# Planned cost of plain tap transfers halved for products 1 and 3, and twenty idle transposes ahead of the first product

## The chip, the cores and the metric

The kernel runs on one core of one Trainium2 chip. The metric is the device time in microseconds (us) of one execution. Engines are named as in the profile: PE is TensorE (matmuls; PEld its weight loads), DVE VectorE, ACT ScalarE, POOL GpSimd, SP SyncE, which issues most transfers. GpSimd also issues the transfers that add into their destination.

## What is computed

A pre-norm transformer block on x of 2 sequences by 1024 tokens by 1024 channels, in float32:

```
x = x + attention(layernorm(x))
x = x + ffn(layernorm(x))

attention(h):  h -> convolution over tokens, width 3, 1024 -> 768 channels
               split into q, k, v of 256; 16 heads of 64; causal softmax
               inside blocks of 128 tokens; out projection; 256 -> 1024
ffn(h):        h @ W_base.T + b_base + four gated low-rank experts
```

The change lies wholly in the first stage, the layer norm and the convolution, which takes the first 235 us of the 770.

## The kernel before, in words

**The convolution as six products.** Four neighbouring output tokens are computed together from six combinations of input tokens, so the convolution becomes six matrix products, numbered v = 0 to 5. Product v multiplies a combination of the tokens (called `v` in the trace, 128 channels by 512 token groups) with a combination of the three taps of the filter (called `u`, 128 by 768). Products 0 and 5 use one tap as it is. Products 1 and 2 share a combination of all three taps, and so do 3 and 4. The products run in the order 0, 5, 1, 2, 3, 4. Each walks over eight blocks of 128 input channels, here called steps d = 0 to 7, and in each step over six blocks of output channels.

**Three matmuls for one.** Each operand is split into a high and a low part, and `three` (line 137) adds high x high, high x low and low x high. The high part comes from ACT, the low part from DVE: `u_hi` (line 441) and `u_lo` (line 445) for taps, `v_hi` (line 500) and `v_lo` (line 504) for tokens. A step is 18 matmuls. Since a step's first two matmuls use only the high part of the tap, PE can begin a step and then wait for `u_lo`.

**How the taps of products 1 and 3 are made.** `load_g` (lines 414 to 416) issues two plain transfers on SP's queue, 384 KB each. For product 1, `sum_g` (line 423) then adds the second and the third tap onto the first in two transfers on POOL's queue, the second waiting for the first. `combine` (line 431 for product 1, lines 435 and 436 for product 3) turns the two tiles into the taps of two products on DVE; `u_hi` and `u_lo` follow. For product 3 one `sum_g` follows after `scale_g` on ACT.

**How the tokens of products 1 to 4 are made.** `tokens_sum` (lines 487 to 490) makes both token combinations for two steps at once. It is four DVE instructions in a row; in the planner it is one piece of 4.7 us.

**The order is planned when the program is built.** Each piece of work is an `Op` with an engine, a planned duration, a due time, a lead, the pieces it comes after, and a lag before its result counts (3.3 for transfers). `trace` (line 289) is a list scheduler: again and again it takes, over all engines, the piece that can start first. On one engine it goes through the pieces by due time and keeps the earliest start, so a piece that is due earlier loses to one that can start sooner. A start is the latest of: the engine is free, due minus lead plus the lateness so far (`late`, how far PE's plan has slipped), and the predecessors' ends with their lags. All transfers share one planned engine "DMA", one at a time. Only the order leaves the planner: the program issues the pieces in the order of their planned starts, each engine carries out its own pieces strictly in that order on the chip, and the planned times themselves appear nowhere in the program. Tiles of tags such as `t3` (23 buffers for taps) are handed out in the same order.

**Due times that matter here.** `begin_chunk` (line 751) plans the tap of step d. In the plan, step d of product 1 is due at 97.2 + 4.3 d. From that, `load_g` is due 34.0 earlier with a lead of 6.0, the first sum 28.0 and the second 21.0 earlier without lead, `combine` 9.5, `u_hi` 5.0 and `u_lo` 2.5 earlier. `tokens_sum` for steps d and d+1 is due 9.0 earlier with the large lead of 22.0.

**The start.** `keep_busy` (line 698) issues transposes of the identity into an unused PSUM bank, `idle`. Line 705 runs 64 of them while the first tokens load. Then come 32 transposes of the first four token tiles (`tr`, line 385), then the first product.

Of the kernel before, what the change touches and what calls it, by code (L numbers as in the profile page):

```python
# [39 lines left out]
def preln_block_kernel(  # L40
# [197 lines left out]
    def bank(name):  # L238
        return ps_m.tile([P, JN], F32, tag="m", name=name)
# [393 lines left out]
    DVE, ACT, PE, DMA = "DVE", "ACT", "PE", "DMA"  # L633

    def load(due, lead, f, *args, takes=1.1, after=()):
        return Op(DMA, takes, due, lead, after, lambda: f(*args), lag=3.3)
# [11 lines left out]
    seen = {}  # L648

    def turn(i, h):  # L650

        due = at[0]
        if h == 0:
            how = HOW[i]
            if how == "scalar":
                o = Op(ACT, 1.3, due - 8.0, 8.0, [loaded[i]], partial(ln_sum, i))
                o = Op(ACT, 1.2, due - 6.0, 8.0, [o], partial(ln_square, i))
                o = Op(DVE, 0.1, due - 4.5, 8.0, [o], partial(ln_variance, i), lag=1.8)
            else:
                lag = 1.0 if how == "vector" else 1.8  # L660
                o = Op(DVE, 1.6, due - 5.5, 8.0, [loaded[i]], partial(ln_stats, i), lag=lag)
            e, us = (DVE, 0.75) if how == "vector" else (ACT, 1.15)
            seen[i] = Op(e, us, due - 2.2, 8.0, [o], partial(ln_scale, i))
        o = Op(
            PE, TR, due, 6.0, [seen[i], banks[-2] if len(banks) > 7 else None],
            partial(transpose, i, h),
        )
        if (i, h) == (8, 0):

            gone["even"] = Op(  # L670
                DMA, 0.01, due - 2.0, 50.0, [seen["tr", j, 1] for j in range(8)], even_tokens
            )
        after = [o] + ([gone["even"]] if i > 7 else [])
        seen["tr", i, h] = o
        banks.append(Op(ACT, 0.52, due + TR, 8.0, after, partial(transposed, i, h)))
        at[0] += TR
        seen[i, h] = banks[-1]

    def weights_due(v, d, due, after):
        o = Op(ACT, 0.76, due - 5.0, 12.0, [after], partial(u_hi, v, d))  # L680
        return Op(DVE, 0.89, due - 2.5, 12.0, [o, after], partial(u_lo, v, d))
# [16 lines left out]
    def keep_busy(n):  # L698
        if not idle:
            idle.append(bank("idle"))  # L700
        for _ in range(n):
            nc.tensor.transpose(idle[0][:, :P], ident, ident)
# [7 lines left out]
    def evacuated(v, c, due):  # L710
        o = gone[v, c] = Op(ACT, 0.55 if v < 4 else 0.85, due, 3.0, [last], partial(evacuate, v, c))
        gone["m", v, c] = load(due, 3.0, spill, v, c, after=[o], takes=0.7)

    for q, (v, n, dc) in enumerate(units):
        base = 0 if v == 0 else 8
        took = [seen.get((base + 4 * n + i, dc // 4)) for i in range(4)]
        if None in took:
            for i in range(4):
                turn(base + 4 * n + i, dc // 4)
            took = [seen[base + 4 * n + i, dc // 4] for i in range(4)]  # L720
        due = at[0]
        o = Op(DVE, 1.28, due - 5.5, 9.0, took, partial(unit_sum, q))
        o = Op(ACT, 0.55, due - 3.5, 9.0, [o], partial(unit_hi, q))
        side = Op(DVE, 0.64, due - 1.5, 9.0, [o], partial(unit_lo, q))
        for i in range(2):
            d = dc + i
            if n == 0:
                if v == 5:
                    gs[5, d] = load(at[0] - 12.0, 12.0, load_g, 5, d)
                ready[v, d] = weights_due(v, d, at[0], gs[v, d])  # L730
            for c in range(NCC):
                after = [last, side, ready[v, d]]
                if v == 5 and n == 0 and d == 0:
                    after.append(gone[0, max(0, c - 1)])
                last = Op(
                    PE, HALF / NCC, at[0], 6.0, after, partial(multiply_unit, q, i, c), lag=0.0
                )
                at[0] += HALF / NCC
            for j in between.get((q, i), []):
                turn(*j)  # L740
        if (n, dc) == (1, NDC - 2):
            for c in range(NCC):
                evacuated(v, c, at[0] + 0.1 * c)
# [6 lines left out]

    def begin_chunk(v, d, due):
        if v == 1:
            o = load(due - 34.0, 6.0, load_g, v, d, takes=2.2)
            for k in (1, 2):
                o = load(due - 35.0 + 7.0 * k, 0.0, sum_g, v, d, k, takes=2.2, after=[o])
            o = Op(DVE, 0.9, due - 9.5, 9.0, [o], partial(combine, v, d))
        elif v == 3:
            o = load(due - 28.0, 6.0, load_g, v, d, takes=2.2)
            o = Op(ACT, 0.76, due - 21.0, 0.0, [o], partial(scale_g, v, d))
            o = load(due - 21.0, 0.0, sum_g, v, d, 0, takes=2.2, after=[o])  # L760
            o = Op(DVE, 1.8, due - 9.5, 9.0, [o], partial(combine, v, d))
        if v in (1, 3):
            gone["g", v, d] = gone["g", v + 1, d] = o
        ready[v, d] = weights_due(v, d, due, gone["g", v, d])
# [16 lines left out]
    for v, dc in [(v, dc) for v in (1, 2, 3) for dc in range(0, NDC, 2)] + [(4, 0), (4, 2)]:  # L781
        if (v, dc) == (2, 0):

            for r in range(4):
                load(
                    at[0] + r, 3.0, nc.sync.dma_start, mask[r::4], causal[ts(r, P // 4)],
                    after=[last],
                )
            Op(DVE, 1.0, at[0], 3.0, [last], gather_experts)
        if (v, dc) == (3, 0):  # L790
            Op(ACT, 0.3, at[0], 3.0, [last], router_bias)
        side = begin_step(v, dc, at[0])
        for d in (dc, dc + 1):
            begin_chunk(v, d, at[0])
            for c in range(NCC):
                last = product(v, d, c, side)
        if dc == NDC - 2:
            for c in range(NCC):
                evacuated(v, c, at[0] + 0.1 * c)

    sides = {}
    for dc in (4, 6):
        sides[dc] = begin_step(4, dc, at[0])
        for d in (dc, dc + 1):
            begin_chunk(4, d, at[0])
# [5 lines left out]
    for c in range(NCC):  # L811
# [7 lines left out]
        o = Op(DVE, 2.7, at[0] + 1.0, 6.0, [got, gone[4, c]], partial(tokens_join, 0, c))  # L819
        o = Op(ACT, 0.6, at[0] + 4.0, 6.0, [o], partial(tokens_hi, 0, c))  # L820
# [432 lines left out]
    d = {}  # L1253
# [364 lines left out]
```

## Time and profile before

| | |
|---|---|
| median of 3 runs | 773.37 us (772.95 to 774.4) |
| the profiled execution's own time | 771.87 us |
| its span, first to last instruction | 770.1 us |
| PE busy | 757.3 us, 98% of the span |
| DVE, ACT, POOL busy | 71%, 52%, 20% |
| mean granted PE clock | 0.996 |
| first stage ends, first `pq` matmul | 234.93 us |

A profile line such as `L445 DVE TENSOR_TENSOR u<-g,u ... x1` names the source line, the engine, the operation and output <- inputs, then shapes and count. In a timeline the first two numbers are the start and the duration in us, and a bracket at the end gives the idle time before the piece and who ended it. "Granted clock" is the share of full clock that the chip's throttle gave PE. Durations of PE instructions contain their pipeline's drain, so neighbours overlap.

### The profile page before, as it was taken

The page shows a single profiled execution, that of the slowest core. Times are in us where ns is not written, and L with a number is a line of the kernel's source. Part 1 is how long each engine was busy: PE and PEld are TensorE (multiplying, and loading weights), DVE is VectorE, ACT ScalarE, POOL GpSimd, SP SyncE. Part 2 cuts the span into 40 slices and gives each one's busy share as a digit, 9 for nine tenths or more (in the row PEclk, how much of TensorE's full clock was granted, in tenths as well). Part 3 has the DMA queues.
Part 4 walks back from the last instruction along what each step waited for, and adds up shares of the span by engine and source line. Part 5 has one row for each costly group of instructions (what it writes and reads, how often), then busy time and mean ns, then how long its engine had stood idle before and what let it go on. Part 6 is the DMA issues. An engine that isn't in the chain of part 4 may idle for free.

```text
span 770.1 us, 13080 instructions
## 1 busy us (share of the span) xinstructions
PE 757.3 (98%) x4928; PEld 676.8 (88%) x4928; DVE 545.8 (71%) x1027; ACT 401.3 (52%) x1015; POOL 157.5 (20%) x138
## 2 busy tenths in 40 slices
PE   6999999999999999999999999999999999999998
PEld 6999978888888888888888887889999999999997
DVE  7788899799667899787787788687444454444532
ACT  6888344564746988888777989832101010110110
POOL 3224322210000304111213013532112111221000
PEclk9999999999999999999999999999999999999999
DMA  9937993996752111030131646750223112311011
GB/s 344 360 102 204 240 259 84 289 292 131 237 156 83 42 54 31 22 117 23 40 94 52 184 154 221 269 234 28 91 74 110 54 55 91 129 55 55 29 55 54
DMA packets 53662, 100.17 MB, mean 130 GB/s; under 512 B 4526, under 2 KB 23742, under 8 KB 53600
## 3 DMA queue, kind: packets, MB, share of 16 engines
q1 hardware_dynamic: 49872, 89.35, 33.4%
q0 software_dynamic: 3728, 10.00, 7.2%
q8 instruction: 38, 0.62, 0.3%
q14 instruction: 24, 0.20, 0.1%
HBM read 73.12 MB, written 26.21 MB: 129 GB/s over the span
## 4 chain that ended last, share of the span: by engine, by line
PE 91%; DVE 6%; issue 2%; DMA 1%; ACT 1%; POOL 0%; SPq 0%; DVEq 0%
PE py L140 24%; PE pm L140 22%; PE pq L140 11%; PE pp L140 6%; PE pw L140 5%; PE pv L140 5%; PE s L901 4%; PE po L965 4%; PE pt L948 4%; PE trx L1145 2%; PE tr L385 1%; PE py L1229 1%; DMA xt<-in_x 1%; DVE vkeep L489 1%; DVE lnst L132 1%
## 5 line engine op out<-in xcount | busy, mean ns | idle before, releaser
L140 PE MATMUL pm<-v,u 128*128 128x256 f32 (+1 forms) x1152 | 206.5, 341 | 5.7 <-ACT v L473 3.4
L140 PEld LDWEIGHTS pm<-v,u 128*128 128x128 f32 x1152 | 180.4, 193 | 29.4 <-ACT v L473 3.6
L140 PE MATMUL py<-wb,xT 128*128 128x354 f32 (+3 forms) x576 | 120.4, 327 | 0.0
L140 PE MATMUL py<-wb_wr,xT 128*128 128x354 f32 (+3 forms) x576 | 118.1, 327 | 0.0
L941 POOL TENSOR_TENSOR p<-p,rs 128x1024 f32<-128x1024 f32 x32 | 61.5, 1925 | 255.3 <-DVE rs L937 221.5
L930 ACT ACTIVATE p<-p,nmx 128x128 f32<-128x128 f32 x256 | 99.5, 398 | 2.7 <-DVE nmx L925 2.5
L140 PEld LDWEIGHTS py<-wb_wr,xT 128*128 128x128 f32 x576 | 96.6, 188 | 2.4
L140 PEld LDWEIGHTS py<-wb,xT 128*128 128x128 f32 x576 | 96.6, 189 | 0.1
L140 PE MATMUL pq<-yt,wqk 128*128 128x512 f32 x384 | 94.3, 399 | 0.0
L140 PEld LDWEIGHTS pq<-yt,wqk 128*128 128x128 f32 x384 | 70.8, 188 | 18.4 <-issue 1.5
L1156 DVE TENSOR_TENSOR xT<-trx,xT 128x512 fp32r<-128x512 f32 x32 | 21.0, 686 | 55.9 <-PE trx L1145 49.1
L1108 POOL TENSOR_TENSOR xr<-xr,projb 128x1024 f32<-128x1024 f32 x16 | 38.3, 2393 | 66.6 <-DMA xr<-in_x 66.6
L1152 ACT CAST xT<-trx 128x512 fp32r<-128x512 f32 x32 | 18.6, 588 | 63.7 <-PE trx L1145 36.3
L1193 ACT ACTIVATE al<-lg,nm 128x4 f32<-128x4 f32 x16 | 4.8, 298 | 88.0 <-DVE nm L1188 88.0
L930 ACT ACTIVATION_READ_ACCUMULATOR p<-p,nmx 128x1 f32 x256 | 50.5, 197 | 0.0
L916 DVE TENSOR_TENSOR p<-s,mask 128x512 f32<-128x512 f32 x64 | 41.6, 678 | 8.8 <-PE s L901 8.5
L140 PE MATMUL pw<-oT,wot 128*128 128x512 f32 x192 | 47.6, 396 | 0.0
L140 PE MATMUL pv<-wvt,yt 128*128 128x512 f32 x192 | 46.6, 392 | 0.0
L893 ACT ACTIVATE qk<-pq,bq 128x512 f32<-128x512 f32 x32 | 38.0, 1187 | 13.9 <-PE pq L140 13.6
L140 PEld LDWEIGHTS pw<-oT,wot 128*128 128x128 f32 x192 | 35.9, 188 | 8.4
L140 PEld LDWEIGHTS pv<-wvt,yt 128*128 128x128 f32 x192 | 36.1, 188 | 8.2
L445 DVE TENSOR_TENSOR u<-g,u 128x768 fp32r<-128x768 f32 x40 | 37.4, 953 | 4.3 <-ACT u L441 2.6
(161 smaller groups left out, 1192.4 us busy)
## 6 DMA issues: line engine op xcount, KB each, us to landing
g<-in_conv_w SPq DMA_DIRECT2D x48, 384.0 KB, 7.7
mdr<-m SPq DMA_DIRECT2D x36, 256.0 KB, 3.2
g<-in_conv_w POOLq DMA_DIRECT2D x24, 384.0 KB, 7.7
xt<-in_x SPq DMA_DIRECT2D x16, 512.0 KB, 9.6
xr<-in_x SPq DMA_DIRECT2D x16, 512.0 KB, 4.0
out<-xr SPq DMA_DIRECT2D x15, 512.0 KB, 2.9
ml<-mdr SPq DMA_DIRECT2D x18, 384.0 KB, 4.7
raw_wb<-in_w_base SPq DMA_DIRECT2D x16, 256.0 KB, 9.6
```

The lines of the kernel that those rows point to most:

```text
L140: nc.tensor.matmul(ps, l[a], r[b], start=first and i == 0, stop=last and i == 2)
L445: nc.vector.tensor_tensor(lo, raws.pop((v, dc)), hi, ALU.subtract)
L893: nc.scalar.activation(out, pq, AF.Identity, bias=b_ap[:, hp : hp + 1], scale=sc)
L901: nc.tensor.matmul(s[j][:, b, :], qh[ts(j, DH), ts(b, P)], kh[ts(j, DH), ts(b, P)], start=True, stop=True,)
L916: nc.vector.tensor_tensor(ps[i][0][:, ts(j, NB), :], ss[i][j], mask[:, None, :].to_broadcast([P, NB, P]), ALU.add,)
L930: nc.scalar.activation(p[:, k, :], p[:, k, :], AF.Exp, bias=nmx[:, k : k + 1], accum_out=sm[:, k : k + 1],)
L941: nc.gpsimd.tensor_tensor(p, p, rs[:, :, None].to_broadcast([P, 2 * NB, P]), ALU.mult)
L948: nc.tensor.transpose(pt[:, ts(b, P)], ps[i][0][:, j * NB + b, :], ident)
L965: nc.tensor.matmul(po[ts(j, DH), ts(b, P)], vh[:, b, ds((i % 4) * P + j * DH, DH)], pT[:, j, ts(b, P)], start=True, stop=True,)
L1108: nc.gpsimd.tensor_tensor(xrs[g], xrs[g], pwt["b"], ALU.add)
L1152: nc.scalar.copy(xTs[g][0][:, ts(h, 4), :], trxs[g, h])
L1156: nc.vector.tensor_tensor(lo, trxs.pop((g, h)), hi, ALU.subtract)
```

## The change

Twenty more idle transposes become a planned piece of PE. It comes after the first half of the fourth tile's transposes, is due at 16.9 with a lead of 1.0 and planned at 2.4 us. And the plain transfers of the taps of products 1 and 3 are planned with 1.1 us for each `load_g` in place of 2.2. The transfers themselves stay as they are.

```diff
         due = at[0]
+        if q == 0:
+
+            Op(PE, 2.4, 16.9, 1.0, [seen["tr", 3, 0]], lambda: keep_busy(20))
         o = Op(DVE, 1.28, due - 5.5, 9.0, took, partial(unit_sum, q))
...
     def begin_chunk(v, d, due):
         if v == 1:
-            o = load(due - 34.0, 6.0, load_g, v, d, takes=2.2)
+            o = load(due - 34.0, 6.0, load_g, v, d, takes=1.1)
             for k in (1, 2):
                 o = load(due - 35.0 + 7.0 * k, 0.0, sum_g, v, d, k, takes=2.2, after=[o])
             o = Op(DVE, 0.9, due - 9.5, 9.0, [o], partial(combine, v, d))
         elif v == 3:
-            o = load(due - 28.0, 6.0, load_g, v, d, takes=2.2)
+            o = load(due - 28.0, 6.0, load_g, v, d, takes=1.1)
             o = Op(ACT, 0.76, due - 21.0, 0.0, [o], partial(scale_g, v, d))
```

## The prediction

> **What bounds the kernel now.** I read the page first: PE is busy 757.3 us of a span of 770.1, so all that can be won without removing matmuls are its 12.8 us of idleness, and any time at a reduced clock. Next, who made PE wait, over the whole span:
>
> ```profile
> PE pm L140 <- ACT v L473: 3.4, 1, 3.4
> PE idle L702 <- DVE identr L124: 2.9, 1, 2.9
> PE pm L140 <- DVE u L445: 1.8, 1, 1.8
> PE pm L140 <- DVE v L478: 0.4, 1, 0.4
> PE pt L948 <- ACT qk L893: 0.4, 1, 0.4
> ```
>
> The columns are the waiter, what it waited for, total us, times, longest. Two waits concern the change: 3.4 us ahead of the first product, and 1.8 us for a low tap part in product 1. The windows view then shows what each did to the clock (columns: length, PE busy, granted clock, DMA share, GB/s):
>
> ```profile
> 13.14:16.56 3.42, 2.11 (x20) 1.00 1.02 403
> 16.56:19.97 3.41, 0.88 (x5) 1.00 1.03 404
> 19.97:23.38 3.41, 3.41 (x19) 0.50 1.03 406
> ...
> 112.13:115.54 3.41, 1.58 (x8) 1.00 1.06 265
> 115.54:118.95 3.41, 3.41 (x9) 0.50 1.08 287
> 118.95:122.37 3.42, 3.42 (x16) 1.00 0.79 163
> ```
>
> After each wait the clock is halved for one stretch of 3.41 us. So the 1.8 us wait costs more than itself. The timeline of PE has step 3 of product 1 starting at 112.89 and step 4 at 120.69, 7.80 us apart, where undisturbed steps lie 4.08 apart (108.81 to 112.89, for one): the wait and its half clock cost 3.72 us. Why is that tap late? DVE's timeline:
>
> ```profile
> 102.14 0.95 DVE L445 TENSOR_TENSOR u<-g,u 128x768 fp32r<-128x768 f32 x1
> 103.01 1.22 DVE L487 SCALAR_TENSOR_TENSOR va<-xo 128x1024 f32<-128x1024 f32 x1
> ...
> 107.80 0.95 DVE L431 SCALAR_TENSOR_TENSOR g<-g,g 128x768 f32<-128x768 f32 x1
> 108.67 1.22 DVE L487 SCALAR_TENSOR_TENSOR va<-xo 128x1024 f32<-128x1024 f32 x1
> 109.80 1.22 DVE L488 SCALAR_TENSOR_TENSOR vb<-xe 128x1024 f32<-128x1024 f32 x1
> 111.05 1.23 DVE L489 TENSOR_TENSOR vkeep<-va,vb 128x1024 f32<-128x1024 f32 x1
> 112.31 1.23 DVE L490 TENSOR_TENSOR va<-va,vb 128x1024 f32<-128x1024 f32 x1
> 113.46 0.95 DVE L431 SCALAR_TENSOR_TENSOR g<-g,g 128x768 f32<-128x768 f32 x1
> 114.33 0.95 DVE L445 TENSOR_TENSOR u<-g,u 128x768 fp32r<-128x768 f32 x1
> ```
>
> DVE is never idle here. The combine of step 3 runs at 107.80, but its `u_lo` only at 114.33, behind a whole `tokens_sum` (108.67 to 113.46, for steps 6 and 7, needed some 12 us later) and the combine of step 4. It is an order that is wrong, not an engine short of time.
>
> **Does the halved planning cost change that order?** I work the planner's rule through by hand; its times decide order alone. PE's plan is 4.0 late from the first product on (planned at 19.80, due 15.80). So the releases in step d are 61.2 + 4.3 d for the load, 73.2 + 4.3 d and 80.2 + 4.3 d for the two sums. Before, the planned DMA engine falls behind: the second sum of step 3 ends at 101.8 and counts at 105.1, that of step 4 at 111.7. With 1.1 for each load: load 0 61.2 to 62.3, six spills to 66.5, load 1 to 67.6, load 2 69.8 to 70.9, sum (step 0, first) 73.2 to 75.4, load 3 to 76.5, sum (1, first) 77.5 to 79.7, load 4 to 80.8, then sums (0, second), (2, first), (1, second), (3, first) to 89.6, load 5 to 90.7, sums (2, second), (4, first) to 95.1, load 6 to 96.2, sum (3, second) to 98.4, sum (5, first) to 100.6, load 7 to 101.7, sum (4, second) to 103.9. With the lag, step 3 counts at 101.7 and step 4 at 107.2, 3.4 and 4.5 sooner.
>
> DVE's plan reaches a choice at 102.13. Before, combine 3 was not ready, so `u_lo` of step 2 and `tokens_sum` (4, 5) went first; at 108.62 combine 4 was not ready either, and `tokens_sum` (6, 7) slipped in. Now combine 3 is ready, and due first. The order becomes combine 3, `u_lo` 2, `tokens_sum` (4, 5) to 108.62, then combine 4 (ready at 107.2, due first), `u_lo` 3, `v_lo` (4, 5), `u_lo` 4, and only then `tokens_sum` (6, 7). Had combine 3 missed its choice by its 0.4, combine 4 would still be ahead of `tokens_sum` (6, 7). The order on SP's queue (loads, spills) and on POOL's (sums) comes out as before, so no transfer is moved past another, and tap buffers are handed out as before up to load 7.
>
> **What that is worth.** By the rows, with starts 0.87 apart for a combine or `u_lo`, 1.14 for `v_lo` and 4.79 for `tokens_sum`: from 102.14, combine 3, `u_lo` 2 to 103.88, `tokens_sum` to 108.67, combine 4 to 109.54, `u_lo` 3 done at 110.5. PE runs out of high parts at 113.51, so 3.0 us of cover. `u_lo` 4 is done at 112.5, step 4 starts at 116.97. Late next is step 5: `tokens_sum` (6, 7) ends at 117.2, combine 5 at 118.1, ACT's `u_hi`, DVE's `v_lo` (6, 7), `u_lo` 5 done at about 120.5, where PE asks at 121.05 + 0.45 = 121.5. A cover of 1.0 us, so the wait goes and none takes its place. Of the 3.72 us I take all, less 0.15 for a first touch of that cover: 3.57. Bounds: 0 if an equal wait arises at step 5, 3.72 at most. After product 1 PE has no wait up to 235 us, and what feeds it is itself released by PE (spills, tap buffers), so the gain should pass through. In product 3 the loads are halved too, but PE waits for nothing there: nothing to win. The narrowest cover is step 4 of product 3, whose `u_lo` ends at 184.99 for a need at 185.97 + 0.45: 1.4 us.
>
> **The twenty transposes.** They stand behind the 32 `tr` and before the product, which is planned at 19.80; their own plan is 15.90 to 18.30, so no other plan moves. On the chip the `tr` row has 32 starts 109 ns apart, the last at 14.98: twenty more take 2.18 us, the last drained at 17.43, before the product's 18.65. PE's other work is not delayed, so their cost is zero; were the product ready 1.2 us sooner, it would show. Queued behind them are only products. They keep one PSUM bank occupied longer: the eighth `tr` bank then takes one freed by ACT's first copy (begun at 13.05, 0.6 us each), 1 us before it is needed.
>
> The gain could be the half clock at 19.97. At full clock a matmul of this product takes 0.12 us, at half 0.213: 16 in 3.41 us, which need 1.91 at full clock, so at most 1.5 us. [...] But in the rows a window that is busy for 1.58 of 3.41 us (46%) also lost it. The two drops lie 28 stretches of 3.413 us apart, and counted back the grid starts at 2.90, with the first transpose. On that grid the window 16.56 to 19.97 would be busy 0.88 + 0.87 = 1.75 us, 51%; kept was one at 62% (2.11 of 3.42). 51 is nearer to 46. So I take no gain, and keep 0 and 1.5 as ends. [...]
>
> **The sum.** The profiled execution's own time is 771.87 (span 770.1 plus 1.77 around it); less 3.57 it would be 768.3. The median of the runs is 1.5 above that execution, and I take the gain off it: 773.37 - 3.57 = 769.8.
>
> **The rivals.**
> - *The clock also stays up at the start*: 769.8 - 1.5 = 768.3. For it: 51% lies above 46%, and no gap is over 1.22 us. Against it: the nearer row.
> - *The wait only moves*: the change doesn't do what it says. The transfers are not faster, DMA share is 1.08 in this window, and DVE would wait at a combine whose sum hasn't landed. Software transfers take 7.7 us from issue to landing by the page: the sum of step 4, issued at 98.77, lands at 106.5 for a combine at 108.67; step 3's, issued at 93.78, lands at 101.5 for 102.14. The covers are small, but positive, and 3.0 us lie behind. If a 1.8 us wait with its half clock comes back at step 5: 773.4.
> - *Slower*: in product 3 a combine is ordered so early that DVE waits for a tap, with `u_lo` of step 4 queued behind it. A wait w there costs PE w - 1.4, and 1.7 more once the clock drops (3.41 us at half). It eats the gain from w = 3.3 on. If the combine of step 5 stood right behind its sum's issue, w would be the 7.7 of such a transfer: 6.3 + 1.7 - 3.57 = 4.4, thus 777.8. Against it: that sum is issued at 172.13 and its combine runs at 180.31, 8 us later, and ACT and POOL, which release it, move forward with PE. The attention stage is planned anew from a shifted start, and could reshuffle to the same effect.
>
> **How the numbers follow.** What a measurement of this kernel can tell from no change is about 0.2%, 1.55 us. Order mended, clock drop stays: 769.8, chance 0.47. Both: 768.3, chance 0.25. Wait only moves: 773.4, 0.15. Slower: 777.8, 0.13. So faster 0.72, same 0.15, slower 0.13. The range reaches from 767.6 (both, all of 3.72, and a scatter of 0.5) to 775.0 (the moved wait and the scatter of 1.5 seen in the runs) and leaves out most of the slow case.
>
> **What would show it.** DVE's timeline: `u_lo` of step 3 right behind combine 4, and ahead of the `tokens_sum` for steps 6 and 7. PE's waits: the row for `u L445` gone; steps 3 and 4 of product 1 4.08 apart; granted clock 1.00 from 112 to 122; the first `pq` near 231.2 instead of 234.93. The start: twenty `idle` between `tr` and `pm`, first `pm` still near 18.65, and the clock of 19.97 to 23.38 decides the 1.5. I would be wrong if DVE shows idle time before a combine, or if a wait over 1 us appears at step 5 or in product 3.

## The result and the profile after

The median is 767.82 us in 4 runs (767.46 to 768.99), against 773.22 in 4 runs before (772.95 to 774.4): a ratio of 0.993 with an interval of 0.9913 to 0.9947. The forecast was 769.8 in a range of 767.6 to 775.0, so the median lies inside, but only 0.2 above the lower end: 5.4 us were gained where 3.6 were forecast. The profiled execution took 767.54 us, 4.33 less than the one shown before. A later batch of the same two kernels gave 767.93 (9 runs) against 772.04 (44 runs), ratio 0.995, 0.9932 to 0.9968.

PE's waits over the whole span of the changed kernel, in the profiled execution (waiter, releaser, total us, times, longest):

```profile
PE idle L702 <- DVE identr L124: 2.9, 1, 2.9
PE pm L140 <- ACT v L473: 0.9, 1, 0.9
PE pt L951 <- ACT vh L872: 0.6, 1, 0.6
PE pt L951 <- ACT qk L896: 0.5, 1, 0.5
PE pm L140 <- DVE v L478: 0.3, 1, 0.3
```

The row for `u L445`, 1.8 us before, is gone. The wait ahead of the first product has shrunk from 3.4 to 0.9, because the twenty transposes now stand in it; the product still starts at 18.64:

```profile
15.35 2.35 PE L702 MATMUL idle<-identr 128*128 128x128 f32 x20
18.64 0.38 PE L140 MATMUL pm<-v,u 128*128 128x256 f32 x1 [0.95 <-ACT v L473]
```

A new 0.6 and a 0.5 in place of 0.4 stand in the attention stage. DVE's timeline in product 1, where the low part of step 3's tap was late:

```profile
100.52 0.95 DVE L431 SCALAR_TENSOR_TENSOR g<-g,g 128x768 f32<-128x768 f32 x1
101.39 0.95 DVE L445 TENSOR_TENSOR u<-g,u 128x768 fp32r<-128x768 f32 x1
102.26 1.22 DVE L487 SCALAR_TENSOR_TENSOR va<-xo 128x1024 f32<-128x1024 f32 x1
...
107.05 0.95 DVE L431 SCALAR_TENSOR_TENSOR g<-g,g 128x768 f32<-128x768 f32 x1
107.92 0.95 DVE L445 TENSOR_TENSOR u<-g,u 128x768 fp32r<-128x768 f32 x1
108.78 1.22 DVE L504 TENSOR_TENSOR v<-va,v 128x1024 fp32r<-128x1024 f32 x1
109.92 0.95 DVE L445 TENSOR_TENSOR u<-g,u 128x768 fp32r<-128x768 f32 x1
110.79 1.22 DVE L487 SCALAR_TENSOR_TENSOR va<-xo 128x1024 f32<-128x1024 f32 x1
```

From the top: combine 3, `u_lo` 2, `tokens_sum` for steps 4 and 5, combine 4, then `u_lo` 3 at 107.92, `v_lo`, `u_lo` 4, and only then `tokens_sum` for steps 6 and 7. PE asks for `u_lo` 3 at about 111.7 and no longer waits. SP and POOL issue their work in the same order as before; PE has twenty more instructions. And the clock at both places (length, PE busy, granted clock, DMA share, GB/s):

```profile
13.67:17.08 3.41, 3.41 (x33) 1.00 1.03 407
17.08:20.50 3.42, 2.13 (x16) 1.00 1.02 397
20.50:23.91 3.41, 3.41 (x31) 1.00 1.03 411
111.20:115.28 4.08, 4.08 (x19) 1.00 1.09 269
115.28:119.36 4.08, 4.08 (x19) 1.00 1.07 252
```

Full clock throughout, where before two stretches of 3.41 us stood at 0.50.

Where the time went, by laying the same matmul of both traces side by side: PE is 1.60 us ahead after the first 36 matmuls of product 0 (23.66 against 25.26) and stays so, within 0.03, up to step 3 of product 1; 5.35 ahead from step 4 of product 1 to the first `pq` (229.58 against 234.93) and on into the attention stage; 4.34 ahead from 470 us to the end. So in this pair of traces the transposes gave 1.6, the mended order 3.7, and 1.0 was given back late.

### The profile page after: what moved, and what is told of

Its sections match the earlier page's. It is cut to its first block, busy times and chain, and to the rows that moved or that the text cites. A ratio compares the mean times of both kernels' runs of the same rounds, so it can differ in the third digit from the quotient of the medians.

```text
span 765.5 us, 13108 instructions
## 1 busy us (share of the span) xinstructions
PE 756.6 (99%) x4948; PEld 676.6 (88%) x4948; DVE 545.0 (71%) x1027; ACT 400.5 (52%) x1015; POOL 157.8 (21%) x138
## 4 chain that ended last, share of the span: by engine, by line
PE 95%; DVE 2%; DMA 1%; ACT 1%; issue 0%; POOL 0%; DVEq 0%
PE pm L140 26%; PE py L140 25%; PE pq L140 11%; PE pp L140 6%; PE pw L140 5%; PE pv L140 5%; PE s L904 4%; PE po L968 4%; PE pt L951 4%; PE trx L1148 2%; PE tr L385 1%; PE py L1232 1%; DVE lnst L132 1%; DMA xt<-in_x 1%; DMA wbd<-raw_wb 0%; DMA raw_pw<-in_proj_w 0%
## 5 line engine op out<-in xcount | busy, mean ns | idle before, releaser
L140 PE MATMUL pm<-v,u 128*128 128x256 f32 (+1 forms) x1152 | 203.1, 337 | 1.3 <-ACT v L473 0.9
L140 PEld LDWEIGHTS pm<-v,u 128*128 128x128 f32 x1152 | 177.9, 190 | 24.2 <-ACT v L473 1.2
L445 DVE TENSOR_TENSOR u<-g,u 128x768 fp32r<-128x768 f32 x40 | 37.5, 951 | 1.4 <-ACT u L441 1.2
```

What stands on the lines that cost most here:

```text
L140: nc.tensor.matmul(ps, l[a], r[b], start=first and i == 0, stop=last and i == 2)
L445: nc.vector.tensor_tensor(lo, raws.pop((v, dc)), hi, ALU.subtract)
```

## The experiments

The theory that the experiments test: the two edits act apart, the costs only through DVE's order at step 3, the transposes only through the clock at the start. The rivals: the gain comes from transfers, not from the order; or from one edit alone; or twenty transposes are more or fewer than are needed. All times are medians in us. Kernels of one batch share the runs before (772.42 in 50 runs, 772.04 in 44, 772.01 in 11). The last column counts executions whose mean granted clock was 0.998 or less: 0.002 of 767 us is 1.5 us lost, about what one stretch of 3.41 at half clock cost in the pair of traces above, 1.60.

| kernel | median, runs | ratio to before, interval | clock 0.998 or less |
|---|---|---|---|
| before | 772.0 to 772.4, 105 | | 101 of 105 |
| costs only | 769.46, 22 | 0.9972 (0.9960 to 0.9985) | 20 of 22 |
| transposes only | 770.20, 22 | 0.9976 (0.9966 to 0.9986) | 4 of 22 |
| order by a lead | 769.56, 13 | 0.9962 (0.9949 to 0.9975) | 12 of 13 |
| changed, 31 transposes | 767.54, 6 | 0.9947 (0.9928 to 0.9966) | 0 of 6 |
| 31, cost 1.4, product 1 only | 767.44, 6 | 0.9943 (0.9921 to 0.9966) | 0 of 6 |
| 31, cost 1.6, product 1 only | 769.38, 20 | 0.9969 (0.9959 to 0.9978) | 1 of 20 |
| 31, product 3 only | 769.52, 16 | 0.9964 (0.9954 to 0.9974) | 0 of 16 |
| changed, again | 767.93, 9 | 0.9950 (0.9932 to 0.9968) | 2 of 9 |
| 31, order by a lead | 767.79, 6 | 0.9944 (0.9928 to 0.9959) | 0 of 6 |
| changed, 8 transposes | 769.08, 6 | 0.9959 (0.9944 to 0.9975) | 4 of 6 |

**Costs only.** The changed kernel without the new `Op`:

```diff
-        if q == 0:
-            Op(PE, 2.4, 16.9, 1.0, [seen["tr", 3, 0]], lambda: keep_busy(20))
```

> The halved planning costs alone, without the twenty transposes. Theory: they only change the order on the vector engine in product 1, which takes away the wait at step 3 and the half clock behind it (3.7 us), so steps 3 and 4 of product 1 start 4.1 us apart, the first pq matmul comes 3.7 us sooner (231.2 in place of 234.9), and the median is 769.5 to 770.5 against 773.2. The half clock ahead of the first product stays. Rival (the gain is the transposes'): the median stays at 773.

769.46, at the lower edge of what the theory has, and 3.0 under before. The wait for `u L445` is gone from the profile. But the profiled execution has no half clock at the start, although PE waits 3.1 us there (its first `pq` comes at 229.99, not at 231.2):

```profile
14.43:17.85 3.42, 1.45 (x14) 1.00 1.05 408
17.85:21.26 3.41, 1.90 (x13) 1.00 1.01 394
21.26:24.67 3.41, 3.41 (x31) 1.00 1.04 417
```

In the trace before, the recorded changes of the clock lie whole lengths of 3.413 us apart (19.97, 23.38, 115.54 and 118.95; between the two drops are 28). That is what grid means below. Where a trace shows no half clock, as here, the stretches are counted on in these lengths, an estimate. Of the three above, one was busy for only 42% (1.45 of 3.42), and the clock behind it stayed at 1.00. In the trace before, one stretch of the gap held 26% (0.88 of 3.41), and the clock behind it was 0.50. And 20 of the 22 executions here had a mean clock of 0.998 or less, two had 1.000. So part of the gain is decided anew in each execution.

**Transposes only.** The new `Op`, with both costs at 2.2.

> The twenty transposes alone, costs as before. Theory: the clock isn't halved after the first product's start, which gives 1.6 us by the first pq matmul (233.3), and the wait at step 3 of product 1 stays: median 771.6. Rival: the throttle's grid of 3.4 us lies differently in each execution, so the halving is only sometimes avoided: the runs fall into two groups about 1.6 us apart, told by their mean clock (0.998 and 0.996).

770.20, 1.4 lower than the theory had it. In 18 of 22 executions the mean clock was 1.000, so no stretch of half clock is seen, not even at the wait of 1.8 us at step 3, which stands unchanged in the profile. The two groups of the rival, at 0.998 and 0.996, are the other four. What the transposes save in one pair of traces is 1.6; by the medians it is 2.2, since without them nearly every execution loses clock (49 of one batch of 50 at 0.998 or less), many of them two or three stretches, by an estimate from the mean clock (22 of the 50 at 0.993: 0.007 of 770 us is 5.4 lost, about 10 us at half clock). The next kernel shows two halved stretches in a row at the start.

**The order mended by another way.** The kernel before with one lead cut, all costs as they were, no transposes. It shares with the changed kernel that `tokens_sum` for steps 6 and 7 comes behind `u_lo` 3 and `u_lo` 4; combine 3 stays behind `tokens_sum` for steps 4 and 5:

```diff
-            kept = Op(DVE, 4.7, due - 9.0, 22.0, banks, partial(tokens_sum, v, dc))
+            kept = Op(DVE, 4.7, due - 9.0, 4.0 if (v, dc) == (1, 6) else 22.0, banks, partial(tokens_sum, v, dc))
```

> The kernel before, all planning costs as before, no transposes; only the lead of the one tokens_sum for steps 6 and 7 of product 1 is cut from 22.0 to 4.0, which puts it behind u_lo of step 3 and u_lo of step 4. Theory (the order on the vector engine is the cause): first pq matmul near 231.2, median about 769.5 to 770. Rival (the taps' data must come sooner, through other places in the transfer queues): nothing is gained, 773, or the wait moves to another tap.

769.56: as much as the halved costs brought. The transfers' planned costs are untouched here, and SP and POOL issue in the order of before up to that step, so DVE's order alone does it. The first `pq` came at 233.35, not at 231.2, mostly because of the start of this one execution:

```profile
15.60:19.01 3.41, 0.85 (x8) 1.00 1.04 407
19.01:22.42 3.41, 2.70 (x11) 0.50 1.02 400
22.42:25.84 3.42, 3.42 (x18) 0.50 1.03 410
25.84:29.25 3.41, 3.41 (x30) 1.00 1.03 411
```

In this execution the clock was 0.50 behind a stretch that was busy for 25%, and still 0.50 behind the next one, busy for 79%: 6.83 us at half clock.

**Thirty-one transposes in place of twenty.**

```diff
-            Op(PE, 2.4, 16.9, 1.0, [seen["tr", 3, 0]], lambda: keep_busy(20))
+            Op(PE, 3.6, 16.9, 1.0, [seen["tr", 3, 0]], lambda: keep_busy(31))
```

> The changed kernel with 31 idle transposes in place of 20, which fill the gap to the first product nearly whole. Theory (what is left of a gap with 20 decides by chance whether the clock is halved): no run is halved at the start, so the runs lie closer together, at 767.5, none near 769. Rival (20 are enough, the slow run had another cause): the same spread as with 20. If the transposes reach beyond the product's readiness, up to 0.3 us is lost.

767.54, no execution at 0.998 or less, and all within 1.4 us. PE's idle time at the start of the first product is down to one piece of 0.34, behind its first matmul. The median is at best 0.4 under the changed kernel, less than these runs can tell. From here on the experiments carry 31 transposes, which keeps the lost clock at the start out of the comparison.

**The changed kernel once more.**

> The changed kernel itself once more, for more executions. Theory: the gap that is left after 20 transposes lets the clock be halved at the start in a minority of executions, so most lie near 767.5 with a mean clock of 0.999 or 1.000 and some near 769 with 0.998. Rival: 20 are enough in every execution, and the median lies at 767.5 with no group above.

767.93; two of nine executions lost clock (768.99 and 770.11), the others lie from 766.93 to 769.04 with 0.999 or 1.000. So twenty protect most executions, not all.

**Eight transposes.** `keep_busy(8)` and a planned cost of 1.0.

> The changed kernel with 8 idle transposes in place of 20, so that 2.5 us of gap are left. Theory (the clock is halved where one stretch of 3.4 us of the throttle's grid holds too little work, and the grid lies differently each time): a good part of the executions is halved at the start, more than with 20 and fewer than with none; mean clocks of 0.998 and 0.999 mixed, median 768 to 769. [...]

769.08, four of six executions at 0.997 or 0.998: with a gap of about 2.3 us (an estimate: 0.95 in the trace with 20, and twelve transposes 109 ns apart) the clock stayed up in only two. Which gap lost it in the four no trace shows, and the clock is not the whole of the 1.2 to 1.5 us above the kernels with 20 and 31. The profiled execution kept full clock and still took 768.93. DVE, ACT, SP and POOL work in the same order as with 20, but PE has two waits more:

```profile
PE pq L140 <- ACT m L516: 0.7, 1, 0.7
PE pm L140 <- DVE u L445: 0.5, 1, 0.5
```

The second is in step 3 of product 3; more on it below.

**How much cost has to go.** 31 transposes, product 3 at 2.2, product 1's load at 1.4 and at 1.6.

> 31 idle transposes, and the load of product 1 planned with 1.4 in place of 1.1; product 3's cost stays at 2.2. In the plan u_lo of step 3 still comes ahead of tokens_sum for steps 6 and 7. Theory (only the order counts): as after_31, 767.5, first pq near 230. Rival (product 3's halved cost brings a part of the gain, or the gain grows with the cost taken off): 768.5 or more.

> The same with 1.6 in place of 1.4: in the plan tokens_sum for steps 6 and 7 now slips back ahead of u_lo of step 3. Theory (a step, not a slope): the wait of 1.8 us at step 3 is back in full, so about 769.6 where the clock stays up there and 771.4 where it is halved; a jump of 2 to 3.7 us for 0.2 of planned cost. Rival (a slope): 768, little above the run with 1.4.

767.44 and 769.38. With 1.6 the plan puts `tokens_sum` for steps 6 and 7 ahead of `u_lo` 3 again, and the wait of 1.8 us is back in the profile; with 1.4 it isn't there. With the planned costs in product 1 at 1.1, 1.4, 1.6 and 2.2 (the last is the next kernel), the medians are 767.54, 767.44, 769.38 and 769.52: a step, not a slope. Its height is 1.9 us, the wait itself: with cost 1.6, step 3 to step 4 takes 6.20 us at full clock (111.69 to 117.89), 2.12 more than undisturbed. The half clock behind the wait, 1.60 us more in the trace before (7.80 in place of 6.20), is seen at most in the 1 of 20 executions that lost clock.

**Product 3 alone.** 31 transposes, product 1's load at 2.2, product 3's at 1.1.

> 31 idle transposes and the halved cost in product 3 alone. Theory: nothing comes of product 3, PE waits for nothing there: the wait at step 3 of product 1 stays, 769.6 to 770.2, as with the transposes alone. Rival: product 3's part brings a gain or a loss of its own, over 0.5 us away from that.

769.52, the same as with 1.6. Product 3's half brings nothing that these runs can tell. Rows of this kernel, first of PE's waits and then of the clock at that wait:

```profile
PE pm L140 <- DVE u L445: 1.8, 1, 1.8
```

```profile
110.95:114.36 3.41, 1.77 (x8) 1.00 1.06 269
114.36:117.77 3.41, 3.21 (x14) 1.00 1.07 283
```

The same wait as before the change, but the stretch that most of it falls in was busy for 52%, and the clock stayed.

**The order by a lead, with 31 transposes.**

> 31 idle transposes, all planning costs as before, and the lead of the one tokens_sum cut to 4.0: the right order by another way, with the clock at the start kept out of the comparison. Theory (the order is the whole of the costs' gain): as after_31 and the run with 1.4, 767.4 to 767.6, against 769.5 for the transposes with the old order. Rival (the costs do something else besides): over 0.7 us away from those.

767.79, within 0.4 of the two kernels that have the order by cost. Its own order costs 0.4 in the trace (4.51 us from step 5 to 6 of product 1 in place of 4.08).

## Why the prediction was right, and where a step failed

**The order: right, step by step.** The order forecast for DVE is the one in the trace, down to `u_lo` 4 ahead of `tokens_sum` for steps 6 and 7. Step 3 to step 4 takes 4.08 us (111.26 to 115.34), the cover at step 5 is 0.9 (`u_lo` 5 ends at 118.94, asked for at 119.87) against 1.0 forecast, no combine of product 1 waits for its sum in this trace (in three others, combine 3 waits 0.2 to 0.4), and SP's and POOL's orders stand. Against the one trace before, the term is 3.72, forecast 3.57. Of the 3.72, 2.12 are the wait and 1.60 the half clock. For the median it was read too large: alone, the costs gave 3.0; with the clock kept up at the start, the order is worth 1.9 (769.4 to 769.5 against 767.4 to 767.8), because then the half clock at step 3 hardly ever came (1 of 36 executions with 31 transposes and the old order had a mean clock of 0.998 or less). So the two edits do not act apart: the medians fell by 3.0 and 2.2 with one of them, but by 4.1 with both (772.04 to 767.93), since with the transposes at the start the half clock at step 3, 90 us later, was mostly gone as well.

**The transposes: the step that failed.** "I take no gain" was wrong; the trace gave 1.6, and the medians of the transposes alone 2.2. The failure is the sentence that the grid starts with the first transpose. It did so in the one trace shown, where the transposes' pace doubled at 6.32. In the trace after it did at 6.84, with the first transpose at 2.91 again, and in the order by a lead the clock fell at 19.01, which is on neither of these two grids. So that agreement was chance, and the computed window, 51% busy, was only one of many. The comparison of 51 with 46 was void as well: 42% was kept (by the estimated stretches of costs only), 46% lost. With a grid that lay differently in each of these three executions, the question is how often a gap costs clock, and the shorter the gap was, the fewer executions lost it (4 of 6 with 8 transposes, 3 of 13 with 20, 1 of 54 with 31). The upper end of 1.5 was too low, too: half clock at the start lasted two stretches in the order by a lead (6.83 us), and one alone cost 1.60 in the pair of traces. With nothing but transposes run, their starts went from 213 to 109 ns apart at 6.32 in the trace before, and with twenty of them in the gap 18 of 22 executions had a mean clock of 1.000 (transposes only).

**The pass-through: nearly right.** The gain was to reach the end whole; 1.0 of 5.35 did not. DVE, ACT, POOL and SP do the attention stage in the order of before, so it was not the replanned attention. PE's two waits at 463 and 464 us are for ACT. What ACT itself waited for, from 440 to 470 us, in the trace after and in the second trace of the same kernel:

```profile
ACT vh L872 <- PE pv L140: 1.5, 1, 1.5
ACT pw L1041 <- DMA raw_pw<-in_proj_w: 1.4, 1, 1.4
```

```profile
ACT vh L872 <- PE pv L140: 1.4, 1, 1.4
ACT pT L961 <- PE pt L951: 1.2, 1, 1.2
ACT pw L1041 <- DMA raw_pw<-in_proj_w: 0.7, 1, 0.7
```

A transfer of the projection's weights arrives a little late for ACT; before, ACT had no such wait, though one of 0.8 for another transfer. PE's waits there sum to 1.2 in one trace of the changed kernel and to 0.5 in the other, against 0.4 before. The other traces fit: where ACT waits 1.7, 1.4, 1.2 and 1.0 for this transfer (order by a lead with 31, changed, transposes only, product 3 alone), PE then waits 1.0, 0.6, 0.5 and 0.2 for `vh`; where ACT waits 0.7 or less, PE doesn't. So part of the gain is given back in some executions and not in others, and not through the halved costs, since the transposes alone have it too. That the transfer is the cause is argued from these rows, not tried by moving it.

**The rivals.** The first, both gains together, came true, and 768.3 was its time. That no gap over 1.22 us is left did not settle it: 0.95 was the longest at the first product in the trace after, and 3 of 13 executions lost clock. That its sum came so near is in part luck: it adds 3.57 for the order, too much at the median, to 1.5 for the clock, too little. No wait moved to another step of product 1.

The slower rival came true in its mechanism, though hardly in its price. One sign named for being wrong was idle time of DVE before a combine. In product 3 it is there, first the line before, then the one after:

```profile
165.49 0.95 DVE L435 SCALAR_TENSOR_TENSOR u<-g,g 128x768 f32<-128x768 f32 x1
```

```profile
165.16 0.96 DVE L435 SCALAR_TENSOR_TENSOR u<-g,g 128x768 f32<-128x768 f32 x1 [2.80 <-issue]
```

The halved cost of product 3 ordered this combine, that of step 3, earlier, and DVE stands idle for 2.80 us before it. The profile names no releaser; two sums issued at 158.21 and 159.68 took 7.1 us to land (median), which would fit. In this trace PE doesn't wait, but `u_lo` of step 3, queued behind, is done only 0.3 us before PE asks for it (176.71 against 176.99), where the forecast had the narrowest cover at 1.4, at step 4. In the trace with eight transposes, of the same order, DVE's idle time there is 3.54, and PE waits the 0.5 shown above for that `u_lo`. By the medians this costs nothing that can be told (767.54 with product 3 halved, 767.44 without), but that half of the edit brings no gain and uses up cover.

**What stays open.** Why the wait at step 3 cost half clock in many executions before (by the mean clocks: 0.993 in 22 of 50, where costs only has none under 0.995), but in one of 36 once the start was kept busy (20 with cost 1.6, 16 with product 3 alone), isn't settled. The traces offer one reading. With the start kept busy and the old order, the estimated stretches cut the wait in two in the two traces whose rows stand here, product 3 alone (above, at 114.36) and transposes only; in the latter it lasts from 112.34 to 114.17, and a stretch ends at 113.57:

```profile
110.15:113.57 3.42, 2.19 (x10) 1.00 1.09 260
113.57:116.98 3.41, 2.81 (x12) 1.00 1.08 254
```

In the trace before, the half clock at the start had put step 3 about 1.6 us later against the grid, and the whole wait (113.50 to 115.33) fell into one stretch, 112.13 to 115.54. That would explain how the start reaches step 3; it is the author's reading, and no run moved the wait by itself to try it. Nor is it settled what decides whether a stretch loses the clock: the share that PE was busy does not separate 42% kept (costs only) from 46% lost (before).

## What to carry to other kernels

Where a list scheduler writes the program, a planned duration is an ordering knob: work through which choice it tips, because the gain comes in a step when one piece of work changes sides (1.9 us between 1.4 and 1.6) and is nothing on either side. Then look at every engine's order after the edit, also where nothing was to be won: product 3 lost cover here. When a short idle gap is followed by half clock, as here one of 3.4 us and one of 1.8, try filling the gap with idle matrix work that ends just before the real work is ready, and fill it whole (here executions at 0.998 or less were 1 of 54 with 31 transposes, 3 of 13 with 20, 4 of 6 with 8). And do not read a clock loss off one trace as a fixed cost: here it came in 49 of 50 executions of the kernel before and in 4 of 22 with the transposes alone, so compare many executions and their mean clocks.

## What the runs showed of the hardware

- In the trace before, the clock was 0.50 from 19.97 to 23.38 and from 115.54 to 118.95: one length of 3.413 us each, 28 lengths from drop to drop. In the order by a lead it was 0.50 for two lengths, 19.01 to 25.84.
- The opening transposes started 213 ns apart at first and 109 ns apart later. The pace changed at 6.32 in the trace before and at 6.84 in the trace after, although the first transpose started at 2.91 in both; the granted clock in the profile reads 1.00 on either side. From 6.32 to the first drop at 19.97 are four lengths of 3.413. The first product starts at 18.65 and 18.64.
- With the order mended and nothing in the gap at the start, 3.1 us in the profiled executions (costs only, order by a lead), 32 of 35 executions had a mean clock of 0.998 or less; with 8 transposes 4 of 6, with 20 in the changed kernel 3 of 13, with 31 1 of 54.
- The kernel before spread from 769.06 to 775.92 in one batch of 50. Its one execution with a mean clock of 1.000 was the one at 769.06.
